# The residual of a gated graph sum taken in by a one on the gates' diagonal, and attention factors packed in 260 columns a head

## The chip, the cores and the metric

The kernel runs on one core of one Trainium2 chip. Its time is the device time of one execution in microseconds (us). Before the change it is 1773.88 us, the median of three runs that lie between 1772.52 and 1774.11. Durations of single instructions come from one profiled execution.

## The reference, cut to what matters

There are 16 graphs of N = 1024 nodes with D = 256 features, and an adjacency of zeros and ones with ones on the diagonal. Each graph goes through two layers.

```python
# layer 0, a gated sum
e0    = leaky(einsum('bid,bjd->bij', x * a0, x))
alpha = sigmoid(where(adj == 1, e0, -max))        # a1..a3 belong to edge kinds 2..4
x     = layernorm(x + einsum('bij,bjd->bid', alpha, x) + bias)
# layer 1, attention with H = 4 heads of F = 64
Wh    = (x @ W).reshape(B, N, H, F)
e     = leaky_relu(e_src[i] + e_dst[j], 0.2)
alpha = softmax(where(adj > 0, e, -1e9))
x     = layernorm(x + elu(einsum('bijh,bjhf->bihf', alpha, Wh)))
```

The exponential of a leaky sum is one of two products: exp(s+d) where s+d is at least zero, exp(0.2 (s+d)) elsewhere. So a head's attention can be had from two sums over j, each with its own factor of j, and the comparison of s with -d tells which edge goes to which sum.

## The kernel before, in words

Nodes are tiled in 8 blocks of 128. `stages` makes the instructions of one graph as about fifty generators, one for each kind of step, and every `yield` ends a step. The steps of all 16 graphs are put in one order by `issue`: each step has a due time in a table (`FIRST` for graph 0, `LAST` for graph 15, `TIMES` for the others), graph b is shifted by b times `PERIOD`, and the steps are issued in the order of these sums. The numbers are only keys for sorting. The engines then run their own lists in this order, and semaphores hold an instruction until its operands are there. Four PSUM banks serve short products (tile names `e`, `pg`, `agg`, `pt`, `pw`, `tot`), and two double banks hold the attention sums (`acc`).

Layer 0 of a graph: `score` multiplies on TensorE, `leak`, `leaky` and `sigmoid` make the gate of the upper triangle, `below` and `lower` mirror it through TensorE, and `upper` (L411, VectorE) masks the upper part row by row in place. `agg` sums over j: for each of the 8 output blocks one product of a matrix of ones with `bias_r` (L418) opens the sum, and 8 products of gate and `xb` (L422) follow. `bias_r` was made once, in `setup`, out of the high and the low part of the bias, since this product reads its operands as fp32r, a rounded form of f32. `residual` (L454, VectorE) adds `xb` to the sum as it leaves PSUM, and the layer norm follows (`moments`, `gathered`, `spread` on GpSimd, `shift`, `norm`).

Layer 1: `project` (L512) gives the features `wh` and the two scores. The chain `top_dve`, `top_pe`, `exps` takes the largest score out and makes the factors `es`. For each head h and each of its two sums s, `product` multiplies `wh` by the factor, `high` (L627, ScalarE) rounds product and factor to fp32r, and `low` (L634, VectorE) writes what the rounding left. All lies in the one buffer `gm`, `[P, H, NB, 2, 2, 66]`: head, block, high or low, sum, 64 columns of product and the factor twice. `pos` (L652, VectorE) compares and masks, and gives the left operand of `acc` (L664), which multiplies it with the 264 columns of one head and block. `acc_low` (ScalarE) and `acc_sum` (L687, VectorE) add high and low parts. `total` (L707) sums the second product over all edges of a row, four heads in four runs of 66 columns. `weigh`, `divide`, `elu` and `join` build the output, a second layer norm ends the graph, and `leave` stores it.

What a step waits for is mostly a buffer: `pos` has six, `acc` two, `gm` one for all graphs, `xb` two. SyncE's queue holds all DMAs in program order.

Of the kernel before, what the change touches and what calls it, by code (L numbers as in the profile page):

```python
# [27 lines left out]
P = 128  # L28
# [8 lines left out]
def shapes(x, a_src):  # L37
    k = Consts()
    B, N, D = x.shape
    H, F = a_src.shape  # L40
    k.B, k.N, k.D, k.H, k.F = B, N, D, H, F
    k.NB, k.DC, k.NH, k.WA = N // P, D // P, N // HALF, D + H
    k.WD = k.WA + H
    k.F1 = F + 2
    return k


def make_constants(nc, k, const, work):
# [14 lines left out]
    k.bias_r = const.tile([P, D], F32R, name="bias_r")  # L63
# [133 lines left out]
def stages(nc, k, pl, b, xg, adjg, outg, sums, span, zinv):  # L197
# [3 lines left out]
    F1, WD = k.F1, k.WD  # L201
# [22 lines left out]
    def setup():  # L224
        if not first:
            yield from (None for _ in range(5))
            return
# [15 lines left out]

        row, low = two("brow")
        nc.sync.dma_start(out=row, in_=bias.partition_broadcast(P))
        for i in range(1, NK):
# [3 lines left out]
        yield  # L250
        high, _ = two("bhigh", F32R)
        nc.scalar.copy(high, row)
        yield
        nc.vector.tensor_tensor(low, row, high.bitcast(F32), ALU.subtract)
        nc.vector.tensor_scalar(low, low, k.ident[:, 1:2], None, ALU.mult)
        nc.vector.scalar_tensor_tensor(
            k.bias_r, high.bitcast(F32), k.ident[:, 0:1], low, ALU.mult, ALU.add
        )
# [155 lines left out]

    def agg():
        for ib in range(NB):
            agg = t["agg", ib] = bank("agg")
            nc.tensor.matmul(  # L418
                agg[:, 0:D], lhsT=k.ones_r, rhs=k.bias_r, start=True, stop=False
            )  # L420
            for jb in range(NB):
                nc.tensor.matmul(  # L422
                    agg[:, 0:D],
                    lhsT=t["gate"][:, jb, ib * P : (ib + 1) * P],
                    rhs=t["xb"][:, jb, :],
                    start=False,
                    stop=(jb == NB - 1),
                )
                if jb == NB // 2 - 1:
                    yield  # L430
            yield
# [16 lines left out]
    def residual():  # L448
        for ib in range(NB):
# [4 lines left out]
            nc.vector.tensor_tensor(y, t["agg", ib][:, 0:D], t["xb"][:, ib, :], ALU.add)  # L454
# [86 lines left out]
    def keep_rows():  # L541
        t["sdram"] = pl.dram.tile([NB * H, P], F32, tag="sdram", name="sdram")
        for half in range(NH):
            rows = slice(half * NQ * H, (half + 1) * NQ * H)
            srow = pl.work.tile([P, 2, 2 * F1], F32, tag="low", name="srow", bufs=2)
# [45 lines left out]
    def exps():  # L591
        es = t["es"] = small("es", 2, NB, H)
        nc.scalar.activation(es[:, 0], t["cm"], AF.Exp)
        nc.scalar.activation(es[:, 1], t["cm"], AF.Exp, scale=SLOPE)
# [7 lines left out]
    def product():  # L602
        for h, s in FACTORS:
# [3 lines left out]
            if last and s:  # L607
                for jb in range(NB):
                    nc.scalar.activation(
                        prod[:, jb, :], t["wh"][:, jb, h * F : (h + 1) * F], AF.Copy,  # L610
                        scale=t["es"][:, s, jb, h : h + 1],
                    )
            else:
                nc.vector.tensor_tensor(
                    prod, t["wh"][:, :, h * F : (h + 1) * F],
                    t["es"][:, s, :, h : h + 1].to_broadcast([P, NB, F]), ALU.mult,
# [3 lines left out]
    def factor(h, s):  # L620
        fac = t["es"][:, s, :, h : h + 1].to_broadcast([P, NB, F1 - F])
        return ((slice(F, F1), fac), (slice(0, F), t["prod", h, s]))

    def high():
        for h, s in FACTORS:
            for cols, val in factor(h, s):
                nc.scalar.copy(pl.gm[:, h, :, 0, s, cols], val)  # L627
            yield

    def low():  # L630
        for h, s in FACTORS:
            for cols, val in factor(h, s):
                hi = pl.gm[:, h, :, 0, s, cols].bitcast(F32)
                nc.vector.tensor_tensor(pl.gm[:, h, :, 1, s, cols], val, hi, ALU.subtract)  # L634
# [23 lines left out]
    def acc():  # L658
        for half, h in HEADS:
            for pair in range(NQ // 2):  # L660
                t["acc", half, h, pair] = pl.ps_u.tile([P, 2, HALF], F32, tag="u", name="acc")
            for jb in range(NB):
                for q in range(NQ):
                    nc.tensor.matmul(  # L664
                        t["acc", half, h, q // 2][:, q % 2, 0 : 4 * F1],
                        lhsT=t["pos", half, h, jb][:, q * P : (q + 1) * P],
                        rhs=pl.gm[:, h, jb].rearrange("p l s f -> p (l s f)"),
# [5 lines left out]
    def acc_low():  # L673
        for half, h in HEADS:
            for pair in range(NQ // 2):
                low = t["low", half, h, pair] = pl.work.tile(
                    [P, 2, 2 * F1], F32, tag="low", name="low", bufs=2
                )
                nc.scalar.copy(low, t["acc", half, h, pair][:, :, 2 * F1 : 4 * F1])  # L679
                yield  # L680

    def acc_sum():
        for half, h in HEADS:
            for pair in range(NQ // 2):
                if h == 0:
                    t["u", half, pair] = pl.us.tile([P, 2, H, 2 * F1], F32, tag="us", name="u")
                nc.vector.tensor_tensor(  # L687
                    t["u", half, pair][:, :, h, :],
                    t["acc", half, h, pair][:, :, 0 : 2 * F1],
# [12 lines left out]
    def total():  # L702
        for ib in TOTALS:
            tot = t["tot", ib] = bank("tot")
            for jb in range(NB):
                for l in range(2):
# [3 lines left out]
                        rhs=pl.gm[:, :, jb, l, 1, :],  # L710
# [9 lines left out]
    def parts(half, pair):  # L720
        return t["u", half, pair].rearrange("p q h (s f) -> p q h s f", s=2)
# [9 lines left out]
    def total_less():  # L731
        for ib in TOTALS[NQ:]:
            u = parts(0, ib // 2)[:, ib % 2, :, 1, :]
            nc.vector.tensor_tensor(u, heads_of(t["tot", ib]), u, ALU.subtract)
# [18 lines left out]
    def weigh():  # L753
        for half, pair in PAIRS:
            ib = half * NQ + 2 * pair
            u2 = parts(half, pair)[:, :, :, 1, :]
            if half:
                nc.vector.tensor_tensor(u2, t["ts", pair], u2, ALU.subtract)
# [4 lines left out]
    def divide():  # L763
        t["rz"] = small("rzs", NB, H)
        for half, pair in PAIRS:
            ib = half * NQ + 2 * pair
            u = parts(half, pair)
            u1 = u[:, :, :, 0, :]
            nc.vector.tensor_tensor(u1, u1, u[:, :, :, 1, :], ALU.add)
            yield  # L770
            rz = t["rz"][:, ib : ib + 2]
            nc.vector.tensor_scalar(rz, u[:, :, :, 0, F], Z_MIN, None, ALU.max)
# [3 lines left out]
            times(u[:, :, :, 0, 0:F], rz)  # L776
# [3 lines left out]
    def join():  # L780
        for half, pair in PAIRS:
            u = parts(half, pair)
            o, ex = u[:, :, :, 0, 0:F], u[:, :, :, 1, 0:F]
# [8 lines left out]
    def elu():  # L792
        for half, pair in PAIRS:
            u = parts(half, pair)
            nc.scalar.activation(u[:, :, :, 1, 0:F], u[:, :, :, 0, 0:F], AF.Exp)
            yield

    def leave():
# [13 lines left out]
        sigmoid=sigmoid(), below=below(), lower=lower(), upper=upper(), agg=agg(),  # L812
# [17 lines left out]
    "xload": [-71.23],  # L830
    "aload": [-103.75, -86.15, -77.72, -57.19, -48.82, -35.24, -20.94, -6.00],
    "cast": [-98.00, -81.30, -61.27, -56.61, -33.26, -15.66, -4.05, 5.78],
    "turn": [-85.08, -73.97, -58.05, -45.90, -25.18, -11.70, -3.58, 12.31],
    "mask": [-79.44, -67.42, -57.07, -36.94, -15.74, -4.70, 4.16, 12.74],
    "setup": [-50.00, -49.00, -48.00, -47.00, -46.00],
    "xt": [-33.59, -31.82, -29.66, -23.47],
    "xtc": [-30.63, -26.14, -24.52, -17.56],
    "xta": [-22.23, -16.07, -11.94, -6.97, -3.31, -0.19, 2.47, 12.73],
    "score": [
        -16.76, -15.29, -13.27, -12.46, -11.47, -7.71, -3.12, -2.68, 0.90, 2.22, 7.95,  # L840
        13.00,
    ],
    "leak": [-16.04, -13.51, -10.58, -8.35, -6.05, -3.68, -0.33, 0.91, 2.02, 10.09, 11.07, 14.17],
    "leaky": [-14.47, -12.97, -10.14, -4.60, -4.39, -2.39, 0.62, 0.92, 4.24, 10.21, 12.13, 25.04],
    "sigmoid": [-9.78, 0.92, 10.01, 10.74, 11.96, 13.37, 37.06, 52.70],
    "below": [-9.53, -2.03, 2.30, 5.61, 10.14, 11.54, 12.50, 30.59, 39.23, 53.84],
    "lower": [-5.37, -1.40, 5.37, 6.48, 11.99, 12.34, 14.77, 33.41, 42.46, 56.55],
    "upper": [12.92, 13.71, 19.19, 28.89, 42.44, 52.20, 55.52, 57.29],
    "agg": [
        14.61, 22.20, 22.23, 22.70, 34.38, 36.09, 36.47, 37.94, 41.01, 44.56, 49.65,  # L850
        53.28, 54.70, 57.81, 58.90, 59.63,
    ],
    "residual": [30.33, 35.23, 37.87, 39.74, 58.93, 59.01, 59.97, 61.18],
    "moments0": [36.23, 37.51, 40.64, 43.34, 59.33, 59.63, 61.16, 62.30],
    "gathered0": [37.65, 39.78, 41.14, 45.41, 59.80, 61.45, 62.80, 64.20],
    "spread0": [47.41, 64.45],
    "shift0": [49.54, 65.26],
    "norm0": [55.34, 56.65, 56.66, 57.82, 65.42, 67.35, 67.45, 68.32],
    "yt": [60.98, 61.24, 70.04, 70.91],
    "ytc": [61.27, 62.49, 71.90, 72.07],  # L860
    "project": [64.75, 67.52, 68.98, 71.47, 72.85, 75.00, 75.19, 76.37],
    "wh": [65.28, 70.52, 71.09, 73.92, 76.46, 77.25, 79.07, 79.11],
    "sources": [76.64, 81.76],
    "rows": [78.98, 97.35],
    "keep_rows": [81.95, 100.14],
    "top_dve": [79.28, 81.84, 82.14, 82.88, 88.45],
    "top_pe": [79.62, 82.52],
    "exps": [89.45],
    "product": [91.63, 91.91, 92.64, 94.83, 101.05, 105.09, 108.06, 112.32],
    "high": [92.22, 93.49, 95.25, 99.68, 104.18, 107.21, 109.04, 112.86],  # L870
    "low": [92.32, 94.50, 100.58, 104.02, 107.97, 110.88, 112.68, 114.35],
    "sload": [88.24, 110.55, 113.86, 125.54, 136.02, 149.85, 160.27, 174.12],
    "pos": [
        95.97, 97.71, 97.86, 98.08, 103.88, 105.39, 109.29, 115.10, 118.25, 118.33,
        118.72, 120.51, 121.34, 122.19, 122.25, 122.75, 127.22, 133.96, 134.09, 134.56,
        137.62, 139.96, 143.17, 144.17, 144.29, 144.32, 144.64, 145.11, 145.13, 145.84,
        149.43, 149.69, 151.18, 151.18, 151.25, 151.27, 151.58, 156.96, 158.44, 159.44,
        159.88, 161.23, 162.72, 163.47, 164.36, 164.69, 165.96, 166.17, 166.95, 167.36,
        170.78, 173.07, 175.22, 176.31, 176.36, 180.19, 180.66, 182.48, 183.50, 183.52,
        188.93, 189.32, 191.48, 194.28,  # L880
    ],
    "acc": [
        98.87, 101.90, 102.34, 104.04, 108.59, 112.11, 112.76, 116.42, 119.96, 120.49,
        121.31, 122.53, 123.40, 123.81, 124.00, 133.89, 141.89, 142.86, 143.29, 143.97,
        144.12, 144.79, 145.08, 145.55, 148.71, 148.79, 148.82, 149.40, 149.48, 149.70,
        149.72, 150.02, 156.71, 157.12, 157.28, 158.08, 158.84, 159.40, 160.65, 161.50,
# [489 lines left out]
```

## Time and profile before

| what | value |
|---|---|
| median of three runs | 1773.88 us |
| the profiled execution itself | 1773.77 us |
| its span, first to last instruction | 1772.0 us |
| TensorE busy | 1719.8 us, 97% |
| VectorE busy | 1622.6 us, 92% |
| ScalarE busy | 1211.6 us, 68% |
| GpSimd busy | 111.1 us, 6% |
| one graph in the steady stretch (from one `pw` group to that of the next graph, 500.16 to 606.42) | 106.26 us |

In a row of the table of groups stand line, engine, operation, output and inputs, shapes and count, then the busy time of the group in us, the mean duration of one in ns, and after the bar the idle time of the engine just before it with what ended it. A busy time counts overlapped time once, so a group's busy time divided by its count is not the distance between two starts: for that the timeline is read, whose first column is the start in us from the span's beginning, and the second how long the merged pieces last together.

### The profile page before, as it was taken

The numbers are of one execution on the slowest core, as the hardware profiler recorded it, in microseconds if no ns is written. First come the engines' busy times: TensorE is split into PE (matmuls) and PEld (weight loads), VectorE is DVE, ScalarE is ACT, GpSimd is POOL, SyncE is SP. The second block draws the span as 40 slices with busy tenths as digits, with TensorE's granted clock in tenths as the row PEclk, the third lists the DMA queues.
The fourth block names the chain that finished last, engine by engine and source line by source line (L and its number), as shares of the span: only waits on it lengthen the run. The fifth ranks groups of instructions, "written<-read, shape, count | busy, mean of one in ns | idle before, by whom it ended". The sixth has DMA issues, their size and how long they took to land.

```text
span 1772.0 us, 29785 instructions
## 1 busy us (share of the span) xinstructions
PE 1719.8 (97%) x10707; PEld 1516.2 (86%) x10707; DVE 1622.6 (92%) x3579; ACT 1211.6 (68%) x2809; POOL 111.1 (6%) x138
## 2 busy tenths in 40 slices
PE   7999999999999999999999999999999999999883
PEld 4789898998979989898998979889898998979883
DVE  4497999999999899999999999899999999999897
ACT  6673957759576684957759486684947759485675
POOL 0000000010000101000010000101000010000100
PEclk9999999999999999999999999999999999999987
DMA  5443324524333343334524334343433425331020
GB/s 158 119 102 90 95 83 96 139 66 117 104 77 116 90 120 96 95 84 103 131 66 118 105 76 114 90 122 93 97 83 102 132 66 137 84 68 53 25 66 26
DMA packets 249275, 168.62 MB, mean 95 GB/s; under 512 B 133280, under 2 KB 232736, under 8 KB 249120
## 3 DMA queue, kind: packets, MB, share of 16 engines
q1 hardware_dynamic: 249120, 166.63, 36.0%
q8 instruction: 87, 1.43, 0.3%
q14 instruction: 68, 0.56, 0.1%
HBM read 118.10 MB, written 17.04 MB: 76 GB/s over the span
## 4 chain that ended last, share of the span: by engine, by line
PE 92%; issue 5%; ACT 1%; DMA 1%; DVE 1%; POOL 0%; SPq 0%; POOLq 0%; ACTq 0%; DVEq 0%
PE acc L664 26%; PE agg L422 25%; PE tot L707 14%; PE e L355 13%; PE pw L512 6%; PE pg L394 3%; PE pt L493 2%; PE pt L319 1%; PE agg L418 1%; ACT a L284 0%; DMA a_sb<-in_L_gnn_a_dram 0%; ACT mT L306 0%; DMA a<-in_adj_dram 0%; PE pbc L586 0%; POOL rstd L464 0%
## 5 line engine op out<-in xcount | busy, mean ns | idle before, releaser
L652 DVE SCALAR_TENSOR_TENSOR pos<-sbc,nd,mT 128x512 fp32r<-128x512 f32 x1024 | 728.8, 740 | 37.8 <-PE acc L664 36.6
L664 PE MATMUL acc<-gm,pos 128*128 128x264 f32 x4096 | 626.2, 298 | 10.3 <-DVE gm L634 6.2
L664 PEld LDWEIGHTS acc<-gm,pos 128*128 128x128 f32 x4096 | 544.7, 190 | 34.1 <-issue 17.6
L422 PE MATMUL agg<-xb,gate 128*128 128x256 f32 x2048 | 473.3, 379 | 0.0
L422 PEld LDWEIGHTS agg<-xb,gate 128*128 128x128 f32 x2048 | 374.4, 190 | 43.8
L707 PE MATMUL tot<-gm,allm 128*128 128x264 f32 x2048 | 323.5, 299 | 5.2 <-ACT gm L627 4.6
L707 PEld LDWEIGHTS tot<-gm,allm 128*128 128x128 f32 x2048 | 282.0, 190 | 10.1 <-ACT gm L627 4.9
L679 ACT COPY low<-acc 128x264 f32<-128x264 f32 x256 | 90.0, 377 | 279.9 <-PE acc L664 279.8
L355 PE MATMUL e<-xT,xTa 128*128 128x512 f32 (+3 forms) x768 | 272.6, 492 | 3.2 <-ACT xTa L343 2.0
L355 PEld LDWEIGHTS e<-xT,xTa 128*128 128x128 f32 x768 | 132.6, 191 | 93.2 <-issue 45.2
L699 ACT CAST allm<-mT 128x512 fp32r<-128x512 uint8 x256 | 156.9, 619 | 24.9 <-PE tot L707 24.4
L484 ACT ACTIVATE y<-y,shift,rstd 128x256 f32<-128x256 f32 x254 | 136.6, 592 | 40.2 <-DVE shift L472 40.1
L284 ACT ACTIVATE a<-a 128x1024 bf16<-128x1024 int32 x128 | 135.6, 1059 | 19.5 <-DMA a<-in_adj_dram 8.1
L306 ACT ACTIVATE mT<-aT 128x1024 uint8<-128x1024 bf16 x120 | 127.1, 1059 | 16.7 <-DMA aT<-a 16.5
L463 POOL TENSOR_SCALAR std<-mv 128x4 f32<-128x4 f32 x64 | 29.7, 463 | 1646.1 <-DVE mv L445 1618.2
L512 PE MATMUL pw<-w_aug,yT 128*128 128x264 f32 x512 | 124.5, 387 | 0.5 <-ACT yT L502 0.5
L375 DVE TENSOR_TENSOR gate<-e,gate 128x512 f32<-128x512 f32 x192 | 103.9, 548 | 12.6 <-ACT gate L367 12.6
L687 DVE TENSOR_TENSOR u<-acc,low 128x264 f32<-128x264 f32 x256 | 104.1, 418 | 7.2 <-ACT low L679 7.1
L512 PEld LDWEIGHTS pw<-w_aug,yT 128*128 128x128 f32 x512 | 92.5, 190 | 13.8 <-ACT yT L502 1.3
L367 ACT ACTIVATE gate<-e 128x512 f32<-128x512 f32 x192 | 92.9, 486 | 15.3 <-PE e L355 15.2
L439 DVE BATCH_NORM_STATS2 st<-y 128x6 f32<-128x256 f32 x256 | 102.2, 413 | 0.8
L411 DVE TENSOR_TENSOR gate<-gate,mT 128x1024 f32<-128x1024 f32 (+7 forms) x128 | 94.8, 749 | 3.3 <-PE pg L394 2.3
(102 smaller groups left out, 1815.5 us busy)
## 6 DMA issues: line engine op xcount, KB each, us to landing
a<-in_adj_dram SPq DMA_DIRECT2D x128, 512.0 KB, 5.0
sbc<-sdram SPq DMA_DIRECT2D x128, 256.0 KB, 4.6
out_dram<-y SPq DMA_DIRECT2D x31, 512.0 KB, 3.5
xb<-in_x_dram SPq DMA_DIRECT2D x15, 1024.0 KB, 5.9
aT<-a SPq DMA_TRANSPOSE x120, 3.1
xb<-in_x_dram SPq DMA_DIRECT2D x2, 512.0 KB, 4.3
sdram<-srow SPq DMA_DIRECT2D x32, 8.0 KB, 1.4
out_dram<-y SPq DMA_DIRECT2D x2, 256.0 KB, 2.3
```

The lines of the kernel that those rows point to most:

```text
L284: nc.scalar.activation(t["a16", ib], t["a32", ib], AF.Copy, accum_out=sums[:, 0, at : at + 1])
L306: nc.scalar.activation(t["mT"][:, :, ib * P : (ib + 1) * P], t["aT", ib], AF.Square, accum_out=sums[:, 1, at : at + 1],)
L355: nc.tensor.matmul(e[:, 0:n], lhsT=t["xTa", jb][:, c, :], rhs=t["xT"][:, c, at : at + n], start=(c == 0), stop=(c == DC - 1),)
L375: nc.vector.tensor_tensor(ge, t["e", jb, at][:, 0:n], ge, ALU.max)
L422: nc.tensor.matmul(agg[:, 0:D], lhsT=t["gate"][:, jb, ib * P : (ib + 1) * P], rhs=t["xb"][:, jb, :], start=False, stop=(jb == NB - 1),)
L484: nc.scalar.activation(y, y, AF.Identity, bias=shift, scale=rstd)
L512: nc.tensor.matmul(pw[:, 0:WD], lhsT=t["yT"][:, c, jb * P : (jb + 1) * P], rhs=k.w_aug[:, c, :], start=(c == 0), stop=(c == DC - 1),)
L652: nc.vector.scalar_tensor_tensor(p_, t["sbc", half, h], t["nd"][:, jb, h : h + 1], t["mT"][:, jb, half * HALF : (half + 1) * HALF], ALU.is ...
L664: nc.tensor.matmul(t["acc", half, h, q // 2][:, q % 2, 0 : 4 * F1], lhsT=t["pos", half, h, jb][:, q * P : (q + 1) * P], rhs=pl.gm[:, h, jb ...
L687: nc.vector.tensor_tensor(t["u", half, pair][:, :, h, :], t["acc", half, h, pair][:, :, 0 : 2 * F1], t["low", half, h, pair], ALU.add,)
L699: nc.scalar.copy(m_, t["mT"][:, j0 : j0 + 4, ib * P : (ib + 1) * P])
L707: nc.tensor.matmul(tot[:, 0 : H * F1], lhsT=t["allm", ib, jb // 4 * 4][:, jb % 4, :], rhs=pl.gm[:, :, jb, l, 1, :], start=(jb == 0 and l = ...
```

## The change

Four things are changed.

1. A new step `self_loop` adds the identity to the diagonal block of the gate in each row block (VectorE, 128x128, in place, 8 a graph). The gated sum then holds x itself. `residual` adds the bias in place of `xb`, from `bias_bc`, the bias copied to all partitions by a DMA. The product with ones at the head of each sum goes, and so does the making of `bias_r` in `setup` (five steps become three).
2. In `gm` a head's block has `E` = 130 columns for the high and 130 for the low part: 64 of the first product, 64 of the second, and each factor once. The two factors change places in `es`. `high` and `low` write both factors of a head in one instruction where they wrote one instruction for each sum.
3. What reads these columns is made narrower: `acc` 260 columns in place of 264, `acc_low` and `acc_sum` 130 for each of two blocks in place of 132, `weigh` and `total_less` 65 a head in place of 66, and the addition in `divide` 64 in place of 66. In `divide` a sum of the two denominators takes the place of a plain lower bound. `total` still reads four runs of 66 columns.
4. All numbers of the three tables are new. `PERIOD` stays.

```diff
     def setup():
         if not first:
-            yield from (None for _ in range(5))
+            yield from (None for _ in range(3))
             return
...
-        row, low = two("brow")
-        nc.sync.dma_start(out=row, in_=bias.partition_broadcast(P))
+        nc.sync.dma_start(out=k.bias_bc, in_=bias.partition_broadcast(P))
...
-        high, _ = two("bhigh", F32R)
-        nc.scalar.copy(high, row)
-        yield
-        nc.vector.tensor_tensor(low, row, high.bitcast(F32), ALU.subtract)
-        nc.vector.tensor_scalar(low, low, k.ident[:, 1:2], None, ALU.mult)
-        nc.vector.scalar_tensor_tensor(
-            k.bias_r, high.bitcast(F32), k.ident[:, 0:1], low, ALU.mult, ALU.add
-        )
...
+    def self_loop():
+        for jb in range(NB):
+            own = t["gate"][:, jb, jb * P : (jb + 1) * P]
+            nc.vector.tensor_tensor(own, own, k.ident, ALU.add)
+            yield
...
     def agg():
         for ib in range(NB):
             agg = t["agg", ib] = bank("agg")
-            nc.tensor.matmul(
-                agg[:, 0:D], lhsT=k.ones_r, rhs=k.bias_r, start=True, stop=False
-            )
             for jb in range(NB):
                 nc.tensor.matmul(
...
-                    start=False,
+                    start=(jb == 0),
...
-            nc.vector.tensor_tensor(y, t["agg", ib][:, 0:D], t["xb"][:, ib, :], ALU.add)
+            nc.vector.tensor_tensor(y, t["agg", ib][:, 0:D], k.bias_bc, ALU.add)
...
-        nc.scalar.activation(es[:, 0], t["cm"], AF.Exp)
-        nc.scalar.activation(es[:, 1], t["cm"], AF.Exp, scale=SLOPE)
+        nc.scalar.activation(es[:, 1], t["cm"], AF.Exp)
+        nc.scalar.activation(es[:, 0], t["cm"], AF.Exp, scale=SLOPE)
...
     def factor(h, s):
-        fac = t["es"][:, s, :, h : h + 1].to_broadcast([P, NB, F1 - F])
-        return ((slice(F, F1), fac), (slice(0, F), t["prod", h, s]))
+        if s == 0:
+            yield slice(2 * F, E), t["es"][:, :, :, h].rearrange("p s b -> p b s")
+        yield slice(s * F, (s + 1) * F), t["prod", h, s]
...
-                nc.scalar.copy(pl.gm[:, h, :, 0, s, cols], val)
+                nc.scalar.copy(pl.gm[:, h, :, 0, cols], val)
...
                     nc.tensor.matmul(
-                        t["acc", half, h, q // 2][:, q % 2, 0 : 4 * F1],
+                        t["acc", half, h, q // 2][:, q % 2, 0 : 2 * E],
                         lhsT=t["pos", half, h, jb][:, q * P : (q + 1) * P],
-                        rhs=pl.gm[:, h, jb].rearrange("p l s f -> p (l s f)"),
+                        rhs=pl.gm[:, h, jb].rearrange("p l f -> p (l f)"),
...
-                        rhs=pl.gm[:, :, jb, l, 1, :],
+                        rhs=pl.gm[:, :, jb, l, F:E],
...
-            nc.vector.tensor_tensor(u1, u1, u[:, :, :, 1, :], ALU.add)
+            nc.vector.tensor_tensor(o, o, u2, ALU.add)
             yield
             rz = t["rz"][:, ib : ib + 2]
-            nc.vector.tensor_scalar(rz, u[:, :, :, 0, F], Z_MIN, None, ALU.max)
+            nc.vector.scalar_tensor_tensor(rz, z1, Z_MIN, z2, ALU.max, ALU.add)
...
 TIMES = {
-    "xload": [-71.23],
+    "xload": [-190.36],
...
-    "upper": [12.92, 13.71, 19.19, 28.89, 42.44, 52.20, 55.52, 57.29],
+    "upper": [-24.74, -21.21, -20.88, -18.06, 1.37, 12.57, 17.16, 22.61],
+    "self_loop": [-22.52, -20.95, -18.10, -17.88, 3.26, 14.07, 18.13, 24.49],
...
-        pl.gm = pl.big.tile([P, H, NB, 2, 2, k.F1], F32R, tag="gm", name="gm")
+        pl.gm = pl.big.tile([P, H, NB, 2, k.E], F32R, tag="gm", name="gm")
```

## The prediction

> **What bounds the kernel now.** I read the busy times first, then the stretches, the groups and the timeline, and last the waits.
>
> ```profile
> PE 1719.8 (97%) x10707; PEld 1516.2 (86%) x10707; DVE 1622.6 (92%) x3579; ACT 1211.6 (68%) x2809; POOL 111.1 (6%) x138
> 531.50:637.80 106.30, 106.30 (x667) 94.12 (x667) 101.11 (x223) 73.88 (x168) 7.00 (x8) 1.00 0.36 100
> 1488.20:1594.50 106.30, 106.30 (x669) 94.41 (x668) 101.34 (x223) 73.81 (x169) 7.00 (x8) 1.00 0.36 91
> 1594.50:1700.00 105.50, 93.67 (x604) 87.69 (x603) 97.68 (x223) 70.29 (x204) 6.22 (x8) 0.95 0.15 44
> 1700.00:1772.00 72.00, 44.95 (x341) 43.44 (x340) 60.09 (x133) 40.44 (x121) 4.59 (x6) 0.83 0.14 42
> ```
>
> The four rows with a colon are stretches of the span: length, then busy time of PE, PEld, DVE, ACT, POOL, then the granted clock. In a steady period (106.3 us for one graph) PE has no gap at all and a clock of 1.00, and DVE is busy 101.1. PE's 52 us of idle time lie at the two ends: some 13 before 106 us, 12 and 27 in the last two rows. So PE sets the pace from about 85 to 1675 us, 15 graphs long, and VectorE stands only 5.2 us a graph behind it. Near the end, where PE is idle in pieces, the last graph's chain over VectorE and ScalarE sets the time.
>
> A busy PE need not be at its peak, so I count starts:
>
> ```profile
> 555.89 2.62 PE L664 MATMUL acc<-gm,pos 128*128 128x264 f32 x20
> 558.35 0.28 PE L418 MATMUL agg<-bias_r,ones_r 128*128 128x256 f32 x1
> 558.47 3.62 PE L422 MATMUL agg<-xb,gate 128*128 128x256 f32 x16
> 561.73 0.47 PE L418 MATMUL agg<-bias_r,ones_r 128*128 128x256 f32 x1
> 562.04 1.24 PE L422 MATMUL agg<-xb,gate 128*128 128x256 f32 x5
> ```
>
> Twenty acc products take 558.35 - 555.89 = 2.46 us, 123 ns each. The trace's mean from start to start, over the steady graphs, is 121.9 ns for acc inside a run (264 columns), 127.2 for tot (264 in four runs), 118.6 for the bias product between acc and agg (256), 215.7 for one of the two passes of an agg product, 222.4 for one of pw's. With e 429, 322, 216 and 111 ns by width (24, 8, 8, 8 passes a graph), 109 for each of 60 transposes, and 0.7 us of small ones, a graph needs 256 x 0.1219 + 128 x 0.1272 + 128 x 0.2157 + 8 x 0.1186 + 32 x 0.2224 + 15.5 + 6.5 + 0.7 = 105.9 us of its 106.26. What is taken off this list comes off the period, so long as VectorE keeps up.
>
> **The change part by part. PE.**
>
> Bias products: 8 a graph. The first costs 558.47 - 558.35 = 0.12 us. One between two agg runs looks dearer (561.73 to 562.04), but the agg pass before it is shown short: 16 agg and one bias take 562.04 - 558.47 = 3.57 us, 16 x 0.2157 is 3.45, so it is 0.12 again. 8 x 0.1186 = 0.95 us a graph, on the path, 15.2 us for 16 graphs.
>
> acc, 264 to 260 columns: acc and bias products differ by 8 columns and 121.9 - 118.6 = 3.3 ns, so 0.41 ns a column and 1.65 ns for four; 256 x 1.65 = 0.42 us a graph. The last graph's acc lies where PE waits anyway, so 15 graphs count: 6.3 us. Here a rule speaks against the change. The Trainium skill ("TensorE: Matmul & The Clock Gate", sections "Back-to-back issue gap" and "LDWEIGHTS") has an isolated product at N/2.4 + 2.5 ns, 112.5 for 264, and says that in a stream of weight load and product both set the spacing, with a load of 128 columns at 128/1.2 = 107 ns. The measured 121.9 lies above the first figure, so the load could be what sets it, and then four columns buy nothing and the sum loses 6.3 us. But both products load 128 columns, and their spacings differ by what 8 columns should cost. I take the slope, and keep zero as the other end.
>
> tot keeps four runs of 66: nothing. Its distance between runs changes; that is not in the trace. Were it laid out like acc it would cost 5.3 ns less, and I allow the same 5.3 more: 128 x 5.3 = 0.7 us a graph either way, 10 us in all. The runs stay as many and as long, so I take zero.
>
> The new order has fewer switches from f32 to fp32r products in PE's list (392 for 507). They are worth nothing: the last agg pass before acc shows 28 ns and the first acc 310, together 338, as 215.7 + 121.9.
>
> Sum for PE: 15.2 + 6.3 = 21.5 us, and a period of 106.26 - 0.95 - 0.42 = 104.9.
>
> **VectorE**, which has to hide all this:
>
> ```profile
> 592.04 0.29 DVE L411 TENSOR_TENSOR gate<-gate,mT 128x128 f32<-128x128 f32 x1
> 592.25 0.20 DVE L774 RECIPROCAL rzs<-rzs 128x8 f32<-128x8 f32 x1
> L634 DVE TENSOR_TENSOR gm<-es,gm 128x16 fp32r<-128x16 f32 x128 | 21.3, 166 | 0.0
> ```
>
> self_loop is 8 in-place additions of 128x128 f32. The nearest row is upper's narrowest, L411 at 128x128: it lasts 0.29 us, but the next instruction starts 0.21 after it. The skill ("VectorE: DVE Perf Modes", section "The TRN2 errata") gives (N + 151)/0.96, 291 ns for 128, and says that the fixed part lies between instructions. The row agrees on the duration, and shows that 80 ns of it overlaps with the next. By the starts self_loop adds 8 x 0.205 = 1.64 us a graph, by the rule 2.33. Removed: four of the eight 128x16 subtractions, 166 ns long and 94 from start to start, 0.38; narrower acc_sum (16 x 4 columns at about 1.05 ns), weigh, total_less and divide, 0.2. The denominator's new operation replaces one as small (161 ns; shift's scalar_tensor_tensor takes 156). Net +1.06 by the starts, 101.1 to 102.2 us; +1.75 by the rule.
>
> So 104.9 - 102.2 = 2.7 us a graph remain for VectorE's waits. What it waits for now:
>
> ```profile
> DVE pos L652 <- PE acc L664: 2.2, 2, 1.3
> DVE shift L472 <- POOL rstd L464: 0.9, 1, 0.9
> DVE span L555 <- ACT wh L524: 0.5, 1, 0.5
> DVE gate L375 <- ACT gate L367: 0.5, 2, 0.2
> DVE y L454 <- PE agg L422: 0.4, 1, 0.4
> DVE u L687 <- ACT low L679: 0.3, 1, 0.3
> ```
>
> (Line, whom it waited for, us in one period, times, longest.) The first is VectorE running ahead of PE: all six pos buffers full. It shrinks by itself once PE is faster. The other five are latencies, 2.6 us. They just fit: 102.2 + 2.6 = 104.8 against 104.9. By the rule's 102.85 they would not, and each graph would lose 0.55 us, 8 us over 15 graphs. I cost the leak at nothing by the starts, and keep 8 us.
>
> **The rest.** ScalarE loses four 203 ns casts a graph and gets narrower copies; busy 74 of 106, nothing. setup drops a cast and three VectorE operations (1.3 us) in a filling stage where VectorE is busy 31 of 60 us; the bias DMA stays one of its kind. Graph 0's self_loop adds 1.6 us of VectorE there: hidden by PE, which runs without a gap from 40 to 69 us; 1.6 us if not. The new waits are two. agg waits for self_loop, and acc, tot and the layer norm's transposes stand behind agg on PE. By the keys a diagonal block is done 3 us or more before the half of agg that reads it, but for the last block: its self_loop (24.49) comes just before the last half of agg (24.56). Eight acc products stand ahead of that half in PE's list, 1 us of work against 0.3 of self_loop; I take nothing, and 0.3 us a graph, 4 us in all, if that cover is gone. xload waits for the last agg of two graphs earlier, since residual no longer reads xb; its key (-190) lies 9 us behind the end of that agg (24.6 - 224 = -199). Behind it on SP stand sbc loads for pos, the next 16 us later (50.8 - 224 = -173) and 4.6 us from landing, so some 11 us of waiting are covered. No issue is added to SP's queue or POOL's in the steady stretch, and I cost both at nothing.
>
> Where VectorE is the tighter one, from 1580 to 1610 (busy 29.97 of 30), the last graph's 8 additions count in full: +1.6 us.
>
> What the new tables do to the two ends, the trace can't tell: PE idles 52 us there. I take no gain, and allow 6 us either way.
>
> **Sum.** The profiled execution took 1773.77 (span 1772.0 and 1.8 around it), 0.1 under the median. 1773.77 - 21.5 + 1.6 = 1753.9, and with the 0.1 that the median lies higher 1754.0 us.
>
> **The rivals.**
>
> A, PE stays the bound, as summed: 1754, with 1748 to 1759 as its own range.
>
> B, VectorE leaks: latency waits grow from 2.6 to about 3.3 us. For it: both steady stretches show VectorE at 95% (101.1 and 101.3 of 106.3). Period 102.2 + 3.3 = 105.5, 15 x 0.6 = 9 us back: 1763.
>
> C, the weight load sets acc's spacing, so narrower columns do nothing: 1754 + 6.3 = 1760. For it the excess of 9.4 ns over the rule, against it the 3.3 ns.
>
> D, slower: VectorE becomes the bound outright. It decides from the point where its latency waits exceed 106.26 - 102.2 = 4.1 us a graph. If all 5.2 us of today's idle time recur, a period is 107.4 and 15 graphs lose 17 us: about 1790. Against it: 2.2 of these 5.2 are waits for PE, which can't recur when VectorE is the late one.
>
> E, the ends get shorter with the new order: more than 6 us of the 52, below 1748.
>
> **How the numbers follow.** A 0.60, B 0.18, C 0.07, D 0.06, E 0.09. Likeliest is A, 1754. B's and C's values are inside a range of 1746 to 1766, E's better half and D outside. A measurement can tell about 0.2%, 3.5 us. Faster: A, B, C, E less the slow end of B, 0.91; same 0.03; slower 0.06, D.
>
> **What would show it.** A period of 104.9 between pw groups, PE without gaps in it, acc at 120.2 ns from start to start, no L418 row; self_loop at 0.28 us long and 0.2 apart; VectorE busy 102.2 a period, with the wait of pos for acc shrunk from 2.2 towards zero. Wrong if PE shows gaps before acc released by pos, which is B or D, or if acc's spacing stays at 121.9, which is C.

## The result

The changed kernel takes 1748.73 us, the median of four runs from 1747.55 to 1750.38, against 1773.45 of the kernel before beside it. The ratio is 0.9862, 95% interval 0.9845 to 0.9879. Forecast were 1754.0 us and a range of 1746 to 1766. The gain is 24.7 us; the forecast had 19.9.

The changed kernel's busy times, from its page, and three stretches of its span (length, then busy time of PE, PEld, DVE, ACT, POOL, granted clock, share and rate of the DMAs):

```profile
PE 1695.6 (97%) x10579; PEld 1494.8 (86%) x10579; DVE 1639.0 (94%) x3640; ACT 1237.6 (71%) x2770; POOL 107.1 (6%) x138
496.02:600.50 104.48, 104.48 (x658) 92.69 (x657) 102.32 (x227) 76.07 (x166) 6.54 (x8) 1.00 0.39 102
1568.60:1680.00 111.40, 99.13 (x636) 92.28 (x636) 104.17 (x235) 74.73 (x215) 5.75 (x8) 0.94 0.18 45
1680.00:1747.00 67.00, 41.66 (x309) 39.63 (x307) 55.59 (x125) 36.47 (x109) 4.13 (x6) 0.83 0.14 41
```

A graph takes 104.48 us, where it took 106.27, and TensorE is still without a gap in it. VectorE is busy 102.3 of these 104.5. Where the whole difference lies is read from the start of the last pw pass of each graph: the first graph's comes at 78.39 us (78.38 before), the last graph's at 1648.82 (1673.69), and 98.23 us follow it (98.31). So all of the 24.9 us of span come from the 15 periods between, and both ends are as long as before.

The same stretch of TensorE's timeline as before (start, length together, count):

```profile
682.78 1.97 PE L658 MATMUL acc<-gm,pos 128*128 128x260 f32 x15
684.58 1.89 PE L415 MATMUL agg<-xb,gate 128*128 128x256 f32 x8
686.12 1.31 PE L658 MATMUL acc<-gm,pos 128*128 128x260 f32 x8
687.27 5.63 PE L415 MATMUL agg<-xb,gate 128*128 128x256 f32 x24
```

No product with ones stands between acc and agg any more. Fifteen acc products take 684.58 - 682.78 = 1.80 us, 120 ns each. By the trace's starts, over eight graphs, TensorE's time for one graph changed so:

| products of a graph | before, us | after, us | difference |
|---|---|---|---|
| 8 with ones | 0.95 | none | -0.95 |
| 256 acc | 31.33 | 30.93 | -0.40 |
| 128 tot | 16.26 | 16.11 | -0.15 |
| e and pg | 18.75 | 18.54 | -0.21 |
| all others | 38.98 | 39.00 | +0.02 |
| sum | 106.27 | 104.58 | -1.69 |

VectorE's waits over the steady stretch of the changed kernel (line, whom it waited for, us in total, times, longest):

```profile
DVE u L681 <- ACT low L673: 14.6, 15, 3.5
DVE gate L364 <- ACT gate L356: 6.1, 13, 0.5
DVE shift L465 <- POOL rstd L457: 4.5, 14, 0.3
DVE pos L646 <- DMA sbc<-sdram: 2.5, 5, 0.7
...
DVE pos L646 <- PE acc L658: 1.3, 2, 0.8
```

The same view of before:

```profile
DVE pos L652 <- PE acc L664: 34.1, 30, 1.9
DVE shift L472 <- POOL rstd L464: 14.2, 15, 1.2
DVE y L454 <- PE agg L422: 8.2, 15, 1.5
DVE gate L375 <- ACT gate L367: 6.8, 25, 1.1
DVE span L555 <- ACT wh L524: 6.4, 13, 0.5
DVE u L687 <- ACT low L679: 5.0, 15, 0.8
```

The wait of pos for acc, VectorE's slack, has all but gone: 1.3 us, before 34.1. The other waits changed too. Shift's for GpSimd is shorter (4.5 us, before 14.2), and y's for agg and span's for wh have nearly left the list, but u's for acc_low has grown from 5.0 to 14.6. The next question is whether the parts or the new order of the steps made the gain.

### The profile page after: what moved, and what is told of

Read it like the earlier page. It is cut to its first block, busy times and chain, and to the rows that moved or that the text cites. A ratio compares the mean times of both kernels' runs of the same rounds, so it can differ in the third digit from the quotient of the medians.

```text
span 1747.1 us, 29629 instructions
## 1 busy us (share of the span) xinstructions
PE 1695.6 (97%) x10579; PEld 1494.8 (86%) x10579; DVE 1639.0 (94%) x3640; ACT 1237.6 (71%) x2770; POOL 107.1 (6%) x138
## 4 chain that ended last, share of the span: by engine, by line
PE 83%; issue 7%; DVE 4%; ACT 3%; DMA 1%; POOL 0%; SPq 0%; POOLq 0%; ACTq 0%; DVEq 0%
PE agg L415 24%; PE acc L658 24%; PE tot L701 13%; PE e L344 11%; PE pw L505 6%; PE pg L383 2%; DVE pos L646 1%; PE pt L308 1%; PE pt L486 1%; DMA sbc<-sdram 1%; DMA aT<-a 0%; ACT mT L295 0%; ACT a L273 0%; DVE gm L628 0%; DVE gate L364 0%
## 5 line engine op out<-in xcount | busy, mean ns | idle before, releaser
L658 PE MATMUL acc<-gm,pos 128*128 128x260 f32 x4096 | 613.3, 293 | 6.5 <-DVE u L681 2.8
L658 PEld LDWEIGHTS acc<-gm,pos 128*128 128x128 f32 x4096 | 538.7, 190 | 19.5 <-issue 3.8
L415 PE MATMUL agg<-xb,gate 128*128 128x256 f32 x2048 | 463.3, 379 | 0.0
L415 PEld LDWEIGHTS agg<-xb,gate 128*128 128x128 f32 x2048 | 380.0, 190 | 46.9 <-DVE gate L407 0.6
L701 PE MATMUL tot<-gm,allm 128*128 128x264 f32 x2048 | 328.4, 297 | 7.1 <-ACT gm L621 5.0
L344 PE MATMUL e<-xT,xTa 128*128 128x512 f32 (+3 forms) x768 | 265.6, 490 | 3.1 <-ACT xTa L332 1.6
L673 ACT COPY low<-acc 128x260 f32<-128x260 f32 x256 | 89.9, 377 | 190.3 <-PE acc L658 190.3
L295 ACT ACTIVATE mT<-aT 128x1024 uint8<-128x1024 bf16 x120 | 127.2, 1060 | 6.4 <-DMA aT<-a 6.3
L364 DVE TENSOR_TENSOR gate<-e,gate 128x512 f32<-128x512 f32 x192 | 104.2, 550 | 21.3 <-ACT gate L356 21.2
L681 DVE TENSOR_TENSOR u<-acc,low 128x260 f32<-128x260 f32 x256 | 102.1, 419 | 16.6 <-ACT low L673 16.6
L432 DVE BATCH_NORM_STATS2 st<-y 128x6 f32<-128x256 f32 x256 | 105.8, 415 | 1.2
L356 ACT ACTIVATE gate<-e 128x512 f32<-128x512 f32 x192 | 90.0, 486 | 14.6 <-PE e L344 14.5
L400 DVE TENSOR_TENSOR gate<-gate,mT 128x1024 f32<-128x1024 f32 (+7 forms) x128 | 95.8, 748 | 4.5 <-PE pg L383 2.4
```

The costliest lines, as they stand in the source:

```text
L295: nc.scalar.activation(t["mT"][:, :, ib * P : (ib + 1) * P], t["aT", ib], AF.Square, accum_out=sums[:, 1, at : at + 1],)
L344: nc.tensor.matmul(e[:, 0:n], lhsT=t["xTa", jb][:, c, :], rhs=t["xT"][:, c, at : at + n], start=(c == 0), stop=(c == DC - 1),)
L364: nc.vector.tensor_tensor(ge, t["e", jb, at][:, 0:n], ge, ALU.max)
L415: nc.tensor.matmul(agg[:, 0:D], lhsT=t["gate"][:, jb, ib * P : (ib + 1) * P], rhs=t["xb"][:, jb, :], start=(jb == 0), stop=(jb == NB - 1),)
L432: nc.vector.bn_stats(st, t["y", half][:, q, :])
L658: nc.tensor.matmul(t["acc", half, h, q // 2][:, q % 2, 0 : 2 * E], lhsT=t["pos", half, h, jb][:, q * P : (q + 1) * P], rhs=pl.gm[:, h, jb] ...
```

## The experiments

Each kernel was run beside the kernel before (1773.3 to 1774.1 us in these series), and the ratios are to it. Busy and idle times of VectorE are means of eight graphs in the middle of the span.

| run | time, us | ratio, 95% interval | period, us | VectorE busy + idle, us |
|---|---|---|---|---|
| before | 1773.5 | 1 | 106.27 | 101.1 + 5.2 |
| changed kernel | 1748.7 | 0.9862 (0.9845 to 0.9879) | 104.48 | 102.2 + 2.4 |
| old_order | 1772.6 | 0.9994 (0.9985 to 1.0002) | 106.38 | 102.8 + 3.7 |
| loop_only | 1781.9 | 1.0045 (1.0028 to 1.0061) | 106.94 | 103.3 + 3.7 |
| pack_only | 1761.0 | 0.9930 (0.9913 to 0.9946) | 105.61 | 100.6 + 5.0 |
| new_order_only | 1778.6 | 1.0027 (1.0018 to 1.0037) | 106.26 | 101.2 + 5.1 |
| wide_acc | 1760.3 | 0.9919 (0.9902 to 0.9936) | 105.06 | 102.3 + 2.7 |
| old_no_loop | 1748.8 | 0.9854 (0.9838 to 0.9871) | 104.69 | 100.6 + 4.1 |
| ones_back | 1762.6 | 0.9932 (0.9915 to 0.9948) | 105.37 | 102.4 + 3.0 |
| dve_plus8 | 1765.5 | 0.9951 (0.9934 to 0.9967) | 105.70 | 104.2 + 1.6 |
| old_pool | 1764.0 | 0.9944 (0.9927 to 0.9961) | 105.82 | 101.6 + 4.3 |
| new_pool | 1746.4 | 0.9844 (0.9828 to 0.9861) | 104.48 | 101.2 + 3.2 |
| pitch272 | 1752.3 | 0.9877 (0.9860 to 0.9893) | 104.70 | 102.3 + 2.4 |

The period is the median distance of the last pw passes; the last column adds up to the mean period, which a longer graph here and there lifts by up to 0.1.

### The parts without the new order

```diff
 # old_order: the changed kernel with before's tables, and in each of them
+    "self_loop": [key of upper + 0.001, ...],
```

> The changed kernel with the tables of before; each self_loop step stands just behind its upper step. Theory A (TensorE's list sets the pace, each part is worth the starts it takes off, and the order is worth about 0.3 us a graph): a period of 104.8 us, 1752 to 1754 us in all. If the order is worth nothing: 104.5 and 1749. Theory B (VectorE's latency waits of 2.6 us a graph no longer fit in the old order): a period of 105.3 or more, 1760 us or more, with gaps of TensorE before acc that pos ends.

Measured: 1772.6 us, a period of 106.38. All three parts together, without the new tables, are worth about nothing (the interval takes in no change). Theory A is out. The sign of theory B is there, gaps of TensorE before acc that pos ends, though the time is far above its 1760. TensorE's longest wait in the steady graphs, and a place from VectorE's timeline:

```profile
PE acc L658 <- DVE pos L646: 5.8, 24, 0.3
```

```profile
678.06 0.68 DVE L400 TENSOR_TENSOR gate<-gate,mT 128x512 f32<-128x512 f32 x1
678.78 0.29 DVE L407 TENSOR_TENSOR gate<-gate,ident 128x128 f32<-128x128 f32 x1
678.99 0.42 DVE L389 TENSOR_TENSOR gate<-pg,mT 128x256 f32<-128x256 f32 x1
```

In this order each addition of self_loop (L407) stands right behind the upper (L400) that writes what it reads, and it starts some 35 ns after that upper has ended (678.06 + 0.68 to 678.78). The third row reads nothing of the addition and starts some 80 ns before it ends (678.99, where the addition ends at 679.07). So each addition takes about 0.32 us of VectorE's time here in place of 0.205, by an estimate from these starts, and the eight take 2.6 us a graph.

```diff
 # loop_only: the kernel before with self_loop, bias_bc and residual as in the change,
 # without bias_r and its product; tables of before with self_loop behind upper
```

> The kernel before with part 1 alone (self_loop, bias by VectorE, no product with ones), tables of before. Theory A: eight starts of 119 ns less a graph, a period of 105.3 us, 15 us less than before, 1759 us. Theory B: VectorE is at 102.7 us and its waits of 2.6 just fill 105.3; it leaks if they grow, 1763 us or more.

Measured: 1781.9 us, 8 us slower than before, with a period of 106.94. TensorE's list is 0.95 us a graph shorter, but it now waits. A stretch, VectorE's waits of one period, and the longest waits of TensorE and of its weight loads over the steady graphs of loop_only:

```profile
612.55:719.43 106.88, 106.43 (x658) 93.06 (x657) 103.26 (x232) 73.85 (x169) 7.12 (x8) 1.00 0.39 100
```

```profile
DVE shift L466 <- POOL rstd L458: 0.9, 1, 0.9
DVE pos L646 <- PE acc L658: 0.8, 1, 0.8
DVE span L549 <- ACT wh L518: 0.5, 1, 0.5
DVE gate L365 <- ACT gate L357: 0.5, 2, 0.2
DVE u L681 <- ACT low L673: 0.3, 1, 0.3
```

```profile
PE acc L658 <- DVE pos L646: 3.3, 15, 0.2
...
PEld acc L658 <- DVE pos L646: 9.4, 24, 0.5
```

VectorE is busy 103.3 us and idle 3.7. Four of its waits are those of before (0.9, 0.5, 0.5, 0.3), and pos still waits 0.8 us for acc, although TensorE waits for pos elsewhere in the period. One place shows how self_loop gets through. VectorE and TensorE of loop_only in order of time, and below it the same place before the change:

```profile
663.07 0.82 DVE L401 TENSOR_TENSOR gate<-gate,mT 128x640 f32<-128x640 f32 x1
...
663.93 0.29 DVE L408 TENSOR_TENSOR gate<-gate,ident 128x128 f32<-128x128 f32 x1
664.25 2.12 PE L658 MATMUL acc<-gm,pos 128*128 128x264 f32 x16
...
665.80 4.05 DVE L646 SCALAR_TENSOR_TENSOR pos<-sbc,nd,mT 128x512 fp32r<-128x512 f32 x6
...
666.60 0.75 PE L658 MATMUL acc<-gm,pos 128*128 128x264 f32 x4 [0.23 <-DVE pos L646]
667.19 5.34 PE L416 MATMUL agg<-xb,gate 128*128 128x256 f32 x24
```

```profile
660.05 0.82 DVE L411 TENSOR_TENSOR gate<-gate,mT 128x640 f32<-128x640 f32 x1
...
662.17 2.62 PE L664 MATMUL acc<-gm,pos 128*128 128x264 f32 x20
662.45 4.06 DVE L652 SCALAR_TENSOR_TENSOR pos<-sbc,nd,mT 128x512 fp32r<-128x512 f32 x6
```

The six pos start at 665.80, which is 2.73 us after upper (663.07). Before the change the same two stand 2.40 us apart (660.05 and 662.45). The same four instructions stand between them in both kernels; the 0.33 us more are the addition at 663.93. The acc products run out of pos tiles, and the next acc starts at 666.60 when pos has written one. Before the change the same 20 acc products run through without a wait.

```diff
 # old_no_loop: old_order, and
     def self_loop():
         for jb in range(NB):
-            own = t["gate"][:, jb, jb * P : (jb + 1) * P]
-            nc.vector.tensor_tensor(own, own, k.ident, ALU.add)
             yield
```

> The changed kernel with the tables of before and without self_loop: the residual x of layer 0 is left out. The run old_order had TensorE wait for pos and for self_loop, 1.5 us a graph over its list. If the 8 additions on VectorE (1.64 us a graph) are what the old order has no room for, these waits go: a period of 104.9 us, 1752 us. If it is something else in the old order, such as the earlier release of xb or the bias, the period stays at 106.4 and the time at 1772.

Measured: 1748.8 us and a period of 104.69. Its stretch:

```profile
602.00:706.69 104.69, 104.69 (x658) 92.56 (x657) 100.58 (x220) 73.37 (x165) 7.12 (x8) 1.00 0.40 102
```

TensorE has no gap again. Eight small additions on VectorE cost the old order 1.7 us a graph, 24 us in all: the same tables without them reach the changed kernel's time. The waits that go are those for pos; for self_loop itself, which the expectation names as well, no wait stands in TensorE's list of old_order.

### The order and the packing alone

```diff
 # new_order_only: the kernel before with the new tables, self_loop's row left out,
 # five steps of setup at the places of the three
```

> The kernel before with part 4 alone: the new tables, 264 columns, product with ones, xb added by VectorE. If the order has a worth of its own: the waits of pg for the sigmoid go, 106.0 us a graph, 1769 us. If it is only room for self_loop: 1773, as before. If the new order is made for the other parts and harms without them (xb is held longer, since VectorE reads it): above 1776.

Measured: 1778.6 us, slower by 5, with the period as it was. The loss lies at the ends: the first graph's last pw pass comes at 82.3 us (78.4 before) and the last period is 108.6 (106.8). So the new order has no worth of its own. Together with old_order: the parts without the order give 1 us, the order without the parts costs 5, and both give 25.

```diff
 # pack_only: the kernel before with gm as [P, H, NB, 2, 130] and all that reads and writes it
 # as in the change; layer 0, setup and tables as before
```

> The kernel before with part 2 and 3 alone (260 columns a head), tables and product with ones as before. By the slope of columns (theory A): acc at 120.2 ns from start to start, a period of 105.8 us, 6.5 us less than before, 1767 us. If the weight load sets acc's spacing (rival C): 121.9 ns still and no gain, 1773 us.

Measured: 1761.0 us, 13 less, twice what was expected. The period is 105.61, shorter by 0.66: acc 31.33 to 30.97 (as the slope of columns has it), tot 16.26 to 16.17, and e with pg 18.75 to 18.56. The last is a wait that the forecast had not counted. TensorE's weight loads waited for the sigmoid, before the change and in pack_only, over the same stretch:

```profile
PEld pg L394 <- ACT gate L381: 7.2, 12, 0.6
```

```profile
PEld pg L393 <- ACT gate L380: 5.0, 12, 0.4
```

Twelve times, once a graph, the wait is 0.2 us shorter, as long as one of ScalarE's small casts that are gone (203 ns). That these casts stand before the sigmoid and make it late is inferred from this, not shown by a run of its own. The order alone shortens the wait as well: new_order_only, which has the casts of before, shows over the same stretch

```profile
PEld pg L394 <- ACT gate L381: 4.5, 13, 0.4
```

The rest of pack_only's 13 us is the last period (1.3 us shorter) and what follows it (1.7 shorter).

```diff
 # wide_acc: the changed kernel, 132 columns in place of 130 for each of high and low
-        pl.gm = pl.big.tile([P, H, NB, 2, k.E], F32R, tag="gm", name="gm")
+        pl.gm = pl.big.tile([P, H, NB, 2, k.EP], F32R, tag="gm", name="gm")   # EP = 132
...
-                        t["acc", half, h, q // 2][:, q % 2, 0 : 2 * E],
+                        t["acc", half, h, q // 2][:, q % 2, 0 : 2 * k.EP],
```

> The changed kernel in its new order with acc widened again to 264 columns: two columns of zeros behind the high and two behind the low part of each head and block. Theory A: acc at 121.9 ns, a period of 104.9 us, 6 to 7 us more than the changed kernel, 1755 us. Rival C: no difference, 1749. tot's distance between its runs is again that of before: if tot's 1.1 ns less in the changed kernel comes from the distance, its spacing goes back to 127.0 and the time to 1757.

Measured: 1760.3 us. The period is 105.06, 0.58 more than the changed kernel's: acc 0.40 (121.4 ns inside a run, 119.9 in the changed kernel) and tot 0.17 (back at 127.2). That is 9 us; 2.7 more lie before the first graph's last pw pass (81.10 for 78.39), where this kernel also fills gm with zeros once. The rival that the weight load sets acc's spacing has fallen.

### The two engines one by one

```diff
 # ones_back: the changed kernel, and in agg
+            nc.tensor.matmul(
+                agg[:, 0:D], lhsT=k.ones_r, rhs=k.zero_r, start=True, stop=False
+            )
```

> The changed kernel with a product of ones and zeros put back at the head of each sum; self_loop stays. Theory A: 8 starts of 119 ns more a graph, a period of 105.45 us, 15 us more than the changed kernel, 1763 us. If the product had been hidden, 1749.

Measured: 1762.6 us, 13.9 more, and a period longer by 0.89. The products with ones were on the path. (The profiled execution took 1767.1 us; its first graph is 3.2 us late, the periods are not touched by that.)

```diff
 # dve_plus8: the changed kernel, and in self_loop
             nc.vector.tensor_tensor(own, own, k.ident, ALU.add)
+            nc.vector.tensor_tensor(own, own, k.ident, ALU.max)
```

> The changed kernel with 8 more operations of self_loop's size a graph on VectorE (a maximum of the diagonal block and the identity, which changes nothing): 1.62 us a graph. VectorE is busy 102.35 of 104.48 and its waits that are latencies take 1.5. If busy time and latencies add (as I now think): 104.0 + 1.5 = 105.5, 15 us more, 1764 us. If the latencies shrink when VectorE is late: 104.5 still, 1749 to 1751. If stalls pass back and forth between VectorE and TensorE as in the old order: above 106, 1772 or more.

Measured: 1765.5 us, 16.8 more, with a period of 105.70. A stretch, TensorE's longest wait in the steady graphs, VectorE's waits in one period, and a pair of operations:

```profile
712.31:818.00 105.69, 105.23 (x658) 92.46 (x657) 104.17 (x235) 75.90 (x166) 7.02 (x8) 1.00 0.39 100
```

```profile
PE agg L416 <- DVE gate L408: 6.1, 13, 0.6
```

```profile
DVE gate L364 <- ACT gate L356: 0.5, 1, 0.5
DVE shift L466 <- POOL rstd L458: 0.3, 1, 0.3
```

```profile
648.87 0.28 DVE L407 TENSOR_TENSOR gate<-gate,ident 128x128 f32<-128x128 f32 x1
649.18 0.29 DVE L408 TENSOR_TENSOR gate<-gate,ident 128x128 f32<-128x128 f32 x1
649.39 0.82 DVE L400 TENSOR_TENSOR gate<-gate,mT 128x640 f32<-128x640 f32 x1
```

More work on VectorE now lengthens the period, and TensorE waits for it. The time that was expected, 1764 us, was met in part by luck. The second operation of a pair reads what the first writes, and starts only after it has ended. A pair takes 0.52 us from start to start (648.87 to 649.39), 0.32 more than an addition alone, so 2.5 us a graph were added and not 1.62. Of the 1.5 us of waits that were to stay, the sigmoid's 0.5 and shift's 0.3 did; u's 0.7 for acc_low did not. So that these waits stay whole and add to the busy time is not shown. Of the 2.5 us 1.2 came through; the new order took up some 1.3.

```diff
 # old_pool from old_order, new_pool from the changed kernel
-            nc.vector.tensor_tensor(own, own, k.ident, ALU.add)
+            nc.gpsimd.tensor_tensor(own, own, k.ident, ALU.add)
```

> The run old_order (changed kernel, tables of before) with the 8 additions of self_loop done by GpSimd, which is 7 us busy of 106. If VectorE's time is what the old order lacks, any engine with room will do: a period of 104.7 us and 1749 us, as without self_loop at all, plus what agg waits for a slower GpSimd. If agg's wait for self_loop, wherever it is done, is the cost: 106 us and 1770.

> The changed kernel with self_loop on GpSimd. TensorE's list sets the pace already (104.5 us with no gaps), so VectorE's 1.6 us buy nothing there: 1748 us, within 2 us of the changed kernel; only the ends, where VectorE is the tighter one, can gain, 2 us at most. If VectorE still holds TensorE back in places that the trace doesn't show: below 1745.

Measured: old_pool 1764.0 us, between the two expected values; new_pool 1746.4. In the old order GpSimd gives back about a third of what self_loop costs there. Most of the rest is one wait, in TensorE's list of old_pool, shown with the group of the additions:

```profile
PE agg L415 <- POOL gate L407: 11.4, 13, 1.8
```

```profile
L407 POOL TENSOR_TENSOR gate<-gate,ident 128x128 f32<-128x128 f32 x128 | 89.0, 700 | 1106.8 <-DVE gate L400 587.7 <-PE pg L383 346.1 <-DVE rzs L771 92.3
```

One addition lasts 0.70 us on average on GpSimd, 0.28 on VectorE, and in the old order the first agg follows its self_loop too closely. In the new order self_loop stands earlier and nothing waits for its additions. VectorE is busy 1.0 us a graph less; but TensorE's list sets the period, 104.48 as without it. The 1.0 is less than the 1.6 that the additions took there by their starts: VectorE's shift instructions, for one, last 266 ns on average in new_pool and 156 in the changed kernel. In the old order too VectorE is busy 101.6 us with GpSimd adding, and 100.6 where nobody adds. Why is not shown. Its 1746.4 us (ratio 0.9844, 0.9828 to 0.9861) can't be told from the changed kernel's.

```diff
 # pitch272: the changed kernel
-        pl.gm = pl.big.tile([P, H, NB, 2, k.E], F32R, tag="gm", name="gm")
+        pl.gm = pl.big.tile([P, H, NB, 272], F32R, tag="gm", name="gm")[:, :, :, 0 : 2 * k.E].rearrange(
+            "p h b (l f) -> p h b l f", l=2
+        )
```

> The changed kernel with 12 unused columns behind the 260 of each block in gm, so that blocks lie 1088 bytes apart in place of 1040 and heads 8704 in place of 8320; acc and tot read as many columns in as many runs. If tot's spacing depends on the distance of its four runs (127.0 ns at 8448 bytes, 125.9 at 8320): it changes again, and with it the period, by some 0.1 to 0.2 us a graph, 1746 to 1751 us. If it is the shorter acc beside it that helps tot: 125.9 ns still, 1749.

Measured: 1752.3 us, a period of 104.70. tot takes 16.34 us a graph, 127.6 ns each; acc stays at 119.8 inside a run. tot's spacing follows the layout of gm, at the same number of columns and runs: 125.9 ns with heads 8320 bytes apart, 127.0 to 127.2 at 8448, 127.6 at 8704. Blocks are moved along with heads (1040, 1056, 1088 bytes), and the place where a run begins in its block is not the same in all of them, so which of these acts, and why, stays open.

## Why the prediction was right

It was right in the time and in what bounds the kernel, and one of its steps would have been wrong without the new order.

- **Products with ones, 0.95 us a graph on the path.** Right: 0.95 from the table of starts, 13.9 us when put back. The forecast's 15.2 counted graph 0 too, whose end did not come earlier (78.39 for 78.38).
- **acc, 0.42 us by the slope of columns, zero by the weight load.** Right with the slope: 0.40, and 0.40 when widened again.
- **tot, zero.** Off by 0.15 us a graph, 2.2 us in all, inside the 0.7 allowed. The reason given for an allowance, the distance of the runs, is borne out so far that the layout of gm acts (pitch272).
- **The switches between kinds of product, nothing.** Nothing in the runs speaks against it: what TensorE's list lost is in the rows above.
- **A wait that was not in the sum.** e and pg take 0.2 us a graph less, 3 us in all, and pg's wait for the sigmoid is not among the longest of the changed kernel. ScalarE's casts were costed at nothing because ScalarE is busy 74 us of 106. pack_only has the gain with the old tables, but new_order_only has a shorter wait with the old casts, so how much of it is the casts' stays open.
- **The new waits, agg for self_loop and xload for agg, nothing.** Right: from 104 to 1570 us TensorE's list has two waits, 1.0 us in all, neither of them for self_loop, and its weight loads wait once for it, 0.4 us; pos waits 2.5 us in all for its loads.
- **self_loop, 0.205 us from start to start.** Right in the order that ran: VectorE's busy time was forecast as 102.2 and is 102.2. Two additions, and what all of them cost by duration:

```profile
642.10 0.28 DVE L407 TENSOR_TENSOR gate<-gate,ident 128x128 f32<-128x128 f32 x1
642.29 0.82 DVE L400 TENSOR_TENSOR gate<-gate,mT 128x640 f32<-128x640 f32 x1
643.14 0.29 DVE L407 TENSOR_TENSOR gate<-gate,ident 128x128 f32<-128x128 f32 x1
643.35 0.19 DVE L773 RECIPROCAL rzs<-rzs 128x8 f32<-128x8 f32 x1
...
L407 DVE TENSOR_TENSOR gate<-gate,ident 128x128 f32<-128x128 f32 x128 | 36.1, 283 | 1.1
```

  From 642.10 to 642.29 and from 643.14 to 643.35 are 0.19 and 0.21 us; the duration is 0.283, near the 291 ns of the Trainium skill's rule ("VectorE: DVE Perf Modes", section "The TRN2 errata"), which for the sum is too much here. But 0.205 is not the cost in every place. The second addition stands right behind its upper and starts after that has ended (642.29 + 0.82 to 643.14). Two of eight stand so in the changed kernel, and all eight in old_order, where one takes 0.32 us, more than the rule gives. The forecast read the spacing between instructions that have nothing to do with each other, and did not ask what would stand just before its additions.
- **"The other five are latencies, 2.6 us. They just fit."** Here the argument failed, and the number held by luck. VectorE is idle 2.4 us a graph in the changed kernel, but with other waits than those counted: shift's fell to 0.3, y's and span's are all but gone, u's for acc_low grew. In the order that the waits were read from they did not fit. VectorE is busy 102.8 us in old_order, 0.6 above the forecast, about what eight lost overlaps of 80 ns make, and idle 3.7: four of the five waits at 2.1, a wait of pos for acc of 0.8, and some 0.8 of shorter ones. The forecast let the wait for acc shrink to nothing "once PE is faster", where 0.8 of it stayed, and it left out the short waits. That 102.8 + 3.7 is the measured period proves nothing, as busy and idle time always add up to it. What shows that VectorE decides there, as in rival D, is that TensorE waits for pos and that the period falls by 1.7 us when the additions are left out (old_no_loop).
- **The order, nothing for the period.** Wrong: the new tables were worth 1.9 us a graph to the parts (106.38 to 104.48), and less than nothing without them. They cut VectorE's idle time from 3.7 to 2.4 and its busy time from 102.8 to 102.2. About 0.7 of the 1.9 us is the place of self_loop alone, by an estimate from the starts: six of eight additions no longer stand behind their upper, 0.12 us each. No run has the old tables with the additions in other places, so how much of a new order was needed stays open.
- **The end, +1.6 us for the last graph's self_loop, and the ends' 6 us either way.** What lies before the first graph's last pw pass and behind the last graph's is as long as before. But the last period is 106.70 for 106.76, while the others got 1.8 us shorter: some 1.7 us were lost there, as many as were forecast. That the eight additions did it is not shown. The last period is also longer than the others in new_pool, which has them on GpSimd (105.76 for 104.48), and in new_order_only, which has none (108.55 for 106.26).

So of the 4.8 us by which the gain is larger, e and pg make 3 and tot 2, the bias of graph 0 takes 1 back, and the rest is less than 1 us.

## What to carry to other kernels

When an edit moves work from the engine that sets the pace to the one just behind it, add that engine's busy time and its waits for latencies, all of them and in the order that will run: the sum, not the busy share, has to stay under the new period. Cost each new instruction where it will stand: right behind the one that writes what it reads, it takes more of the engine's time than behind another. A wait read in one order of the work does not hold in another, and an order can be worth nothing or less until the parts need the room that it makes.

## What the hardware showed that was not expected

An in-place addition of 128x128 f32 on VectorE lasts 0.28 to 0.29 us, but takes 0.20 to 0.21 us of the engine's time behind an instruction it does not depend on, and 0.32 right behind the one whose output it reads (old_order, dve_plus8). The spacing of products whose moving operand comes in four runs changes with the layout of that operand (125.9, 127.2 and 127.6 ns for three layouts of the same columns). Idle time of VectorE did not take up all of its own added work: 2.5 us added to 2.4 idle lengthened the period by 1.2. GpSimd needs 0.70 us on average for an in-place addition of 128x128 f32 that VectorE does in 0.28.
